# Four graph layers on one core: layer 1's steps moved by nearly half a period in the written order, the setup split into thirteen placed steps, new orders at both ends

## The chip, the core and the metric

The kernel runs on one core of a Trainium2 chip. The core has a matrix engine (TensorE, PE in the profile; its weight loads are listed as PEld), a vector engine (VectorE, DVE), a scalar engine with function tables (ScalarE, ACT), a general engine (GpSimd, POOL) and SyncE (SP), which here only issues DMA transfers. [...] The metric is the time of one execution on the device in microseconds, as the median of several runs.

## The reference

There are 64 graphs of 256 nodes with 256 features, `x` (64, 256, 256), and an adjacency matrix `adj` of 0 and 1. Four layers follow each other; after each, the sum of input and output is normalized (`_layernorm(x + layer(x))`). Cut to what matters:

```
# layer 0: attention with 4 heads, mask by adj, output projection, layer norm
q, k, v = x @ Wq.T + bq, x @ Wk.T + bk, x @ Wv.T + bv
attn = softmax(where(adj == 0, NEG, q k^T / 8));  out = norm((attn v) @ Wo.T + bo) * gamma + beta
# layer 1: 8 heads whose queries, keys and values are all norm(x), then a two-layer MLP
n = norm(x) * gamma1 + beta1;  x = x + softmax(mask(n n^T / sqrt(32))) n
x = x + gelu((norm(x) * gamma2 + beta2) @ W1 + b1) @ W2 + b2        # W1 is 256 x 1024
# layer 2: Wh = h @ W; scores leaky_relu(s1_i + s2_j), masked softmax, times Wh
# layer 3: scores leaky_relu((h * a0) h^T) where adj == 1, masked softmax, times h
```

## The kernel before

The 64 graphs are worked in 32 groups of two (`G = 2`). The work of a group is written as eleven Python generators, the threads, each of which issues a few instructions and then yields:

- `a` (`thread_a`, L686): loads adjacency and features; ACT makes a bf16 copy `adjb` and a check (`adjb`, `adj`), SP transposes it with four DMA transposes (`adjT`), DVE makes `mask` and the transposed `xT`; then layer 0's projections on PE (`WqT`, `WkT`, `WvT`), the scores (`ps<-qT,kT`, in two row tiles of 64), the exps on ACT (`e<-ps`), the masking on DVE, the products (`pm<-e,v`, in four column tiles of 32) and the row sums (`pm<-ea,ones`), whose reciprocal `zs` DVE takes.
- `u0`, `u1` (L798, one per graph): `zs` goes by DMA to memory (`lines`) and comes back spread over the partitions (`rr`); DVE scales `oT`, PE applies `WoT`, then two normalizations give `z`, layer 1's input, and `xb`.
- `z0`, `z1` (L850): `z` transposed, by a way through memory (`rows`, `blk`, then a DVE transposition into `t`), or on PE where `DIRECT` (L44) names it for a group.
- `b` (L857): layer 1's attention. Its scores are `ps<-t`, in four row tiles of 32; its exps are masked in quarters with a sum; its products are `pm<-e,z`, in four column tiles.
- `w0`, `w1` (L923): normalization, residual and transposition (`yT`).
- `c` (L964): W1 (`pm<-t,L_gnn_W`) and GELU on ACT (`hT<-pm`), in four pairs.
- `o0`, `o1` (L1009): W2 (`pm<-L_gnn_W,hT`), then layers 2 and 3 (`wx`, `ex`, `v,q`, then `pm<-t`, `q`, `xn,q`) and the output.

Which thread goes on next is written by hand. `PLACES` (L46) gives every step a place in periods; group g's copy of it is shifted by g, and all are sorted into one order (L1178). A period is 163 steps. The first 520 steps are replaced by the text `FIRST`, the last 444 by `LAST`: letter and digit are thread and group (counted from eight before the end in `LAST`). The class `InOrder` (L464) ties each instruction to the one recorded before it on its engine, so the written order is the order on every engine; all these instructions carry the line of that helper, L473. ACT's function tables follow from this order too: exp and GELU are in different sets, and the program holds an `ACT_TABLE_LOAD` wherever one follows the other.

Tiles come from pools that reuse a fixed number of buffers (`BUFS`, L45), each waiting for the last reader of what it held. In PSUM there are two score tiles `ps` and four tiles `pm` for everything else.

Constants: six loads stand on ACT's queue at the start. The other seventeen are collected in `later` (L532) and issued on SP by `prepare` (L1090), which runs beside the threads, one step after each of the seven turns in `PREPARE`: two steps with loads; `bop` = Wo applied to the value bias, plus `bo` (needs `WoT`, `bv`, `bo`); the loads of W1 and W2 with the sums for layer 2's vector (`wa`, `wx`); `b2m`; bounds for a check; and last the W1 step, in which PE multiplies W1 with `beta2` (16 products of one column, `pm<-beta,L_gnn_W`) and DVE scales W1 with `gamma2`. Small constants share the buffer of `hT` until group 0's GELU takes it.

Of the kernel before, what the change touches and what calls it, by code (L numbers as in the profile page):

```python
# [8 lines left out]
F32 = mybir.dt.float32  # L9
# [4 lines left out]
ALU = mybir.AluOpType  # L14
AX = mybir.AxisListType

P = 128
N = 256
D = 256
NC = D // P  # L20
# [4 lines left out]
W = D + 4  # L25
DFF = 1024
NF = DFF // P
EPS = 1e-5
SLOPE = 0.2
# [14 lines left out]
DIRECT = {0: ('x', 'z'), 31: ('yT', 'n2', 'n3')}  # L44
BUFS = {'t': 6, 'q': 3, 'k': 2, 'v': 5, 'y': 4, 'z': 4, 'xb': 4, 'both': 2, 'xn': 6, 'mask': 3, 'e': 6, 'x0': 2, 'turned': 1, 'blk': 3, 'oT': 2, 'zs': 2, 'rr': 2, 'xT': 1, 'qT': 1, 'kT': 1}  # L45
PLACES = {  # L46
    "a": (0.00000, 0.26380, 0.44172, 0.77301, 0.77914, 0.78528, 0.80982, 0.85890, 0.87730, 0.95092, 0.96932,
        0.99386, 1.04295, 1.07362, 1.08589, 1.11043, 1.12883, 1.13497, 1.17178, 1.18405, 1.19018, 1.21472,
        1.25767, 1.27607, 1.28221, 1.29448, 1.31902,),
    "u0": (1.33742, 1.34356, 1.34969, 1.40491, 1.41104, 1.49080, 1.54601, 1.56442, 1.60736, 1.68098,),  # L50
    "u1": (1.36810, 1.41718, 1.51534, 1.55215, 1.57055, 1.60123, 1.63190, 1.65031, 1.67485, 1.79141,),
    "z0": (1.61350, 1.66258, 1.69325, 1.72393,),
    "z1": (1.75460, 1.80368, 1.82209, 1.85276,),
    "b": (1.74847, 1.76074, 1.76687, 1.81595, 1.84049, 1.84663, 1.89571, 1.90184, 1.90797, 1.91411, 1.92024,
        1.92638, 1.93865, 1.95705, 1.96319, 1.98773,),
    "w0": (1.93251, 1.94478, 2.01841, 2.02454, 2.06135, 2.14110, 2.22086, 2.30675,),
    "w1": (2.01227, 2.03068, 2.03681, 2.09203, 2.14724, 2.20245, 2.23313, 2.31288,),
    "c": (2.32515, 2.38037, 2.48466, 2.50920, 2.53374, 2.57669, 2.58896, 2.61963,),
    "o0": (2.63804, 2.65644, 2.69939, 2.73620, 2.82822, 2.86503, 2.88957, 3.04908, 3.19632, 3.20859, 3.30061,
        3.33129, 3.37423, 3.38650, 3.39264, 3.42331, 3.43558, 3.46626, 3.47853, 3.52147, 3.58282, 3.62577,  # L60
        3.64417, 3.66871, 3.71779, 3.98159, 4.05521, 4.07975, 4.09816, 4.10429, 4.11656, 4.12270, 4.25153,
        4.59509,),
    "o1": (2.79755, 2.83436, 2.87117, 2.88344, 2.97546, 3.00614, 3.06749, 3.23926, 3.26994, 3.28834, 3.35583,
        3.36196, 3.42945, 3.44785, 3.45399, 3.46012, 3.47239, 3.49693, 3.50307, 3.55828, 3.68712, 3.70552,
        3.71166, 3.73006, 3.74233, 4.15337, 4.15951, 4.16564, 4.17791, 4.22699, 4.24540, 4.52761, 4.53988,
        5.39877,),
}
PREPARE = (8, 14, 26, 50, 70, 85, 100)
FIRST = (
    "a0a0a0a0a0a0a1a1a1a0a0a0a0a0a0a0a0a1a1a0a0a2a0a0a0a0a0a0a0a0a1a0a0a0U0U0U0a1a1U0a1u0u0a2U0U0u0u0U0U0U0Z0Z0u0"  # L70
    "u0u0u0a2Z0Z0U0b0b0b0b0u0z0b0a2z0z0b0z0b0b0b0b0b0b0W0W0a1b0b0b0a1b0a1W0W0W0W0w0u0w0w0w0W0a1a1a1a1a1a1a1a1a1a1"
    "W0a1w0a1a1a1w0w0w0c0a1c0U1U1c0c0U1U1u1U1U1u1u1c0a2a2c0c0c0u1O0O0U1U1U1Z1a2u1Z1u1U1u1u1O0u1o0O0Z1z1z1Z1b1b1b1"
    "O0z1o0o0o0u1z1b1b1b1a2a2b1b1b1b1b1b1O0O0W1W1b1o0a2b1b1a3a3a2a2b1o0O0a2w1W1W1W1o0o0w1w1w1a2a2a3a2a2a2a2a2W1W1"
    "a2a2w1w1w1O0O0a2a2a2W1o0a4o0U2U2w1a2a2u2u2o0o0c1c1O0O0o0o0o0o0o0c1u2c1o0o0o0U2O0O0O0O0U2c1O0O0O0U2U2c1U2U2O0"
    "O0c1c1u2U2Z2O1o0o0o0O1Z2u2u2O0O0o0a3o1U2O0u2u2o0Z2Z2u2O0O1O1z2a3a3b2b2b2o1o1o1a4z2z2b2b2b2z2a3a3a3b2b2b2b2b2"
    "b2b2b2a4a4O0O0W2O1O1W2O1a3a3b2b2o1o0o0a3a3o1W2W2w2W2W2u2w2w2O1w2O0O0a3a3a3a3o1a3W2W2O0O0w2w2w2a3a3a3a3O1o0o0"
    "o1o0o0O1a3a3a3U3U3o1o1a3w2O1a3c2O1U3o1c2o1O1O1O0O0U3U3U3u3u3u3o0o0o1o1o1o1c2c2O1U3U3c2c2O1O1u3U3Z3o1c2u3u3O1"
    "u3u3c2O1O2O2Z3o1u3Z3Z3O1O1u3b3o1o1O1O2O2z3o1O1O1o2O1O0b3b3b3o1o1z3b3O2z3O2O2o1o1b3o2o2a4z3b3a4b3a4O2b3b3b3b3"
    "b3o2a4a4O1O1b3O1O1a4a4W3b3a4U3W3W3W3o2b3w3o2o2O1a4a4a4a4w3w3a5W3O1w3")
LAST = (  # L80
    "a7w5a6o4o3o3O4O3a6a6a6W5W5o4a6o4o4U6U6w5a6u6u6c5c5o4O4U6o4o4o4O4o2o4o4U6U6U6o4o3c5c5c5O4o3O3c5a7o4o4U6U6U6Z6"
    "u6O4O4O4O4O4u6u6u6o4o4c5u6Z6u6c5O5Z6U6Z6b6O4O4o4O4u6z6z6O5b6b6b6u6O5O5O4z6b6o5b6O5O4O4O4o5a7o4o4a7a7z6b6o5o5"
    "b6a7b6b6b6b6W6W6b6a7a7b6a7a7W6W6O5O5b6b6o4o4o5o5o5a7w6w6w6O5a7a7a7a7O4w6a7a7O4O4O4W6W6a7a7a7w6w6o4O5o4o5O4O5"
    "a7a7O4a7a7W6o5o4o4W6w6w6o5o4a7U7o5U7a7U7o5u7u7c6c6U7O5o4o5O4O4U7O5c6u7c6U7o5o5U7U7U7Z7o5u7u7o3O5u7o5o5Z7O5O5"
    "O5u7u7Z7c6o5c6U7c6O5c6u7z7o5o5O6O6O6O5O6z7z7Z7b7b7o6b7b7u7o5O6O5O5O5b7b7O6O5o6o6o6z7b7O6b7b7O4b7b7W7b7O6W7o6"
    "o6o6b7b7o5o5O5O5O5b7b7w7O6W7O6o6w7o5o6o5o5o5w7W7o6O5W7o5o5w7O5w7o4O5o5W7W7O5O5O5O5w7w7O6w7W7c7c7O6O6o6O6O6o6"
    "c7c7o5O6O6c7O5O5o6o6o6o5o6c7c7c7o6o6O7O6O7O7O6O6o7o6O6O6O6O6O7O7o6o6o7o6O6o7O7O7o6o6O6O6o7o7O6O6O7O7o7O6o6O7"
    "O7O6o7o7O6o7o5o7o7O7o7O7O7O6O6O7O7O7o7o7o6o7o7o7o6o6o6o6o6O7o6O7O7O7o7o7O7o7o7o7O7O7O7o7o7o7O7O7O7o6O7O7o7o7"
    "O7o7O7O7o7o7o7o7O7o7o6o7")
LETTERS = dict(a="a", U="u0", u="u1", Z="z0", z="z1", b="b", W="w0", w="w1", c="c", O="o0", o="o1")  # L90
# [358 lines left out]
def usual_input(ctx: ExitStack, tc: tile.TileContext, a: dict, out: bass.AP, flag: bass.AP):  # L449
# [84 lines left out]
    def load(queue, to, of):  # L534
        if queue:
            queue.dma_start(to, of)
        else:
            later.append((to, of))

    def load_rows(name, cols, queue=None):  # L540

        src = a[name]
        t = const.tile([P, src.shape[0] // P, cols], F32, name=name)
        load(queue, t, src.rearrange("(c p) f -> p c f", p=P))
        return t
# [22 lines left out]
    beta0 = load_all(a["L0_gnn_beta"], "beta0", queue=ACT)  # L568
    woT = load_rows("L0_gnn_WoT", D)
    bv = load_column(a["L0_gnn_bv"], D, "bv")  # L570
    bo = load_all(a["L0_gnn_bo"], "bo", 0)

# [4 lines left out]
    gamma0 = load_all(a["L0_gnn_gamma"], "gamma0")  # L577
    beta1r = load_all(a["L1_gnn_beta1"], "beta1r")
    gamma1r = load_all(a["L1_gnn_gamma1"], "gamma1r", 256)
    b2 = load_all(a["L1_gnn_b2"], "b2", 512)  # L580
    gamma1 = load_column(a["L1_gnn_gamma1"], D, "gamma1")
    beta1 = load_column(a["L1_gnn_beta1"], D, "beta1")
    gamma2 = load_column(a["L1_gnn_gamma2"], D, "gamma2")
    beta2 = load_column(a["L1_gnn_beta2"], D, "beta2")
    b1 = load_column(a["L1_gnn_b1"], DFF, "b1")
    a0 = load_column(a["L3_gnn_a0"], D, "a0")
    w1 = load_rows("L1_gnn_W1", DFF)
    w2 = load_rows("L1_gnn_W2", D)
# [500 lines left out]

    def prepare():  # L1090

        for to, of in later[:3]:
            SP.dma_start(to, of)
        yield
        for to, of in later[3:-2]:
            SP.dma_start(to, of)
        yield
# [8 lines left out]
        for to, of in later[-2:]:  # L1106
            SP.dma_start(to, of)
        wa = setup[:, 1280:2304].rearrange("p (s c d) -> p s c d", s=2, c=NC)
        for s in range(2):
            DVE.tensor_tensor(wa[:, s], wx[:, :, 0:D], a12[:, s:s + 1, :].to_broadcast([P, NC, D]), ALU.mult)  # L1110
        DVE.tensor_reduce(wa1, wa, AX.X, ALU.add)
        for k, (s, share) in enumerate(((0, SLOPE - 1.0), (1, SLOPE), (1, 1.0))):
            DVE.tensor_scalar(wx[:, :, D + k:D + k + 1], wa1[:, s, :].unsqueeze(2), share, None, ALU.mult)

        yield
# [15 lines left out]

        yield
# [23 lines left out]
        yield  # L1156

        pm = new(ps_m, [P, NF], F32, "pm", 4)
        for f in range(NF):
            for c in range(NC):  # L1160
                matmul(pm[:, f:f + 1], w1[:, c, f * P:(f + 1) * P], beta2[:, c:c + 1], start=c == 0, stop=c == NC - 1)
        DVE.tensor_tensor(b1, b1, pm, ALU.add)
        for c in range(NC):
            DVE.tensor_scalar(w1[:, c, :], w1[:, c, :], gamma2[:, c:c + 1], None, ALU.mult)
# [7 lines left out]

    def written(text, since):
        return [(since + int(text[k + 1]), LETTERS[text[k]]) for k in range(0, len(text), 2)]

    preparing = prepare()
    groups = [threads_of(g) for g in range(B // G)]
    plan = [(g, n) for _, g, n in sorted((g + t, g, n) for g in range(B // G) for n, ts in PLACES.items() for t in ts)]  # L1178
    head, tail = written(FIRST, 0), written(LAST, B // G - 8)
    for turn, (g, name) in enumerate(head + plan[len(head):len(plan) - len(tail)] + tail):  # L1180
        next(groups[g][name], END)
        if turn in PREPARE:
            next(preparing, END)
    assert next(preparing, END) == END
# [54 lines left out]
```

## Time and profile before

| | before |
|---|---|
| median of three runs | 2473.54 us (2472.14 to 2473.80) |
| the profiled execution | 2474.4 us, span from first to last instruction 2472.5 us |
| PE busy | 2414.1 us (98%), 15888 instructions |
| DVE busy | 2119.0 us (86%) |
| ACT busy | 1510.2 us (61%), among it 65 table loads of 1283 ns |
| POOL busy | 747.2 us (30%) |
| DMA | 229.78 MB, mean 93 GB/s |

How to read it. The page divides the span into 40 slices of 61.8 us and gives each engine's busy share in tenths; PEclk is the share of its full clock that TensorE was granted. Every fp32 matmul of the program appears as two passes, so 16 products are `x32`. A matmul's shape is given as rows * columns of the array and as the size of what streams through: `128*128 128x256` fills the array, `32*128` is one of four row tiles, `128*32` one of four column tiles. Matmul lengths overlap, so durations on PE are best taken from start to start. In a list of waits the columns are who waited, for whom, microseconds in total, times, and the longest. A PE wait is listed only from 0.15 us on.

### The profile page before, as it was taken

Reading aid. Unit: us, or ns where it says so; the run is one execution under the profiler, and the core shown is the slowest. Engines: PE = TensorE matmul, PEld = TensorE weight load, DVE = VectorE, ACT = ScalarE, POOL = GpSimd, SP = SyncE. Lnnn points to the kernel's source line nnn. Section 1 sums busy time; section 2 is a strip of 40 time slices with the busy share of each in tenths; the row PEclk is TensorE's granted clock in tenths of the full one; section 3 lists DMA queues with packets and bytes.
Section 4 is the critical chain, followed back from the end, with each engine's and each line's share of the span. In section 5 each row is a group of like instructions: output and inputs, shape, how many; then the busy total and the mean of one; then the engine's idle time right before and its main releaser. Section 6 shows DMA issues by size and latency. Waiting matters only on the chain.

```text
span 2472.5 us, 48109 instructions
## 1 busy us (share of the span) xinstructions
PE 2414.1 (98%) x15888; PEld 1811.9 (73%) x15888; DVE 2119.0 (86%) x6238; ACT 1510.2 (61%) x2635; POOL 747.2 (30%) x1804
## 2 busy tenths in 40 slices
PE   5899999999999999999999999999999999999997
PEld 3577777777777777787777777777777777777776
DVE  4788888988888988889988889988888988889884
ACT  3456566666666666666666666665666666666654
POOL 0222233323233233233232333232333232333232
PEclk9899999999999999999999999999999999999999
DMA  6235253444443444443444444444444444434321
GB/s 143 46 82 108 61 112 88 92 98 101 96 103 86 92 97 101 101 103 86 91 96 102 103 96 91 89 99 103 103 87 96 92 99 101 106 85 92 81 65 44
DMA packets 903791, 229.78 MB, mean 93 GB/s; under 512 B 707313, under 2 KB 903153, under 8 KB 903537
## 3 DMA queue, kind: packets, MB, share of 16 engines
q1 hardware_dynamic: 902032, 225.73, 41.8%
q8 instruction: 128, 2.10, 0.4%
q14 instruction: 127, 1.03, 0.1%
q10 hardware_dynamic: 1504, 0.92, 0.1%
HBM read 136.07 MB, written 82.05 MB: 88 GB/s over the span
## 4 chain that ended last, share of the span: by engine, by line
PE 72%; ACT 8%; DVE 6%; DMA 5%; SPq 4%; POOL 3%; issue 2%; ACTq 0%; DVEq 0%; POOLq 0%
PE pm L473 65%; PE ps L473 7%; SPq L473 4%; DMA blk<-rows 3%; ACT e L473 2%; ACT adj L473 1%; DVE y L473 1%; DVE e L473 1%; ACT adjb L473 1%; POOL rstd L473 1%; ACT xn L473 1%; DVE st L473 1%; ACT xb L473 1%; POOL nm L473 1%; ACT oT L473 1%
## 5 line engine op out<-in xcount | busy, mean ns | idle before, releaser
L473 POOL TENSOR_SCALAR ve<-mv 128x2 f32<-128x2 f32 x448 | 149.3, 333 | 1613.9 <-DVE mv L473 1104.9
L473 PE MATMUL pm<-L_gnn_W,hT 128*128 128x256 f32 x2048 | 468.0, 382 | 0.0
L473 PE MATMUL pm<-t,L_gnn_W 128*128 128x256 f32 x2048 | 458.2, 379 | 1.6 <-DVE t L473 1.6
L473 ACT ACTIVATE e<-ps 128x1024 f32<-128x1024 f32 x384 | 373.0, 1021 | 126.1 <-PE ps L473 125.4
L473 PEld LDWEIGHTS pm<-L_gnn_W,hT 128*128 128x128 f32 x2048 | 382.0, 190 | 67.0 <-issue 18.9
L473 PEld LDWEIGHTS pm<-t,L_gnn_W 128*128 128x128 f32 x2048 | 386.5, 190 | 53.9 <-DVE t L473 2.1
L473 DVE SCALAR_TENSOR_TENSOR e<-e,mask 128x256 f32<-128x256 f32 x1024 | 364.7, 420 | 12.7 <-ACT e L473 12.4
L473 POOL TENSOR_TENSOR rstd<-ve,mhalf 128x2 f32<-128x2 f32 (+1 forms) x384 | 344.9, 898 | 32.0
L473 ACT ACTIVATE xn<-y,nm,rstd 128x256 f32<-128x256 f32 x256 | 139.5, 593 | 278.0 <-POOL xn L473 223.0
L473 DVE BATCH_NORM_STATS2 st<-y 128x6 f32<-128x256 f32 x640 | 236.3, 411 | 4.7
L473 DVE STREAM_TRANSPOSE t<-blk 128x512 f32<-128x512 f32 x248 | 172.1, 703 | 75.1 <-DMA blk<-rows 74.9
L473 ACT ACTIVATE hT<-pm,b 128x512 f32<-128x512 f32 x256 | 163.9, 676 | 28.5 <-PE pm L473 25.1
L473 PE MATMUL ps<-t 32*128 32x256 f32 x2048 | 156.8, 406 | 5.2 <-ACT t L473 4.0
L473 DVE TENSOR_TENSOR e<-e,mask 128x1024 f32<-128x1024 f32 x128 | 149.7, 1213 | 0.5 <-ACT e L473 0.5
L473 PEld LDWEIGHTS ps<-t 32*128 32x128 f32 x2048 | 100.7, 187 | 61.1 <-ACT qT L473 18.9
L473 DVE SCALAR_TENSOR_TENSOR y<-pm,r,xn 128x256 f32<-128x256 f32 x256 | 123.8, 484 | 9.4
L473 PE MATMUL pm<-wx,t 128*128 128x259 f32 x512 | 127.7, 392 | 2.4
L473 PE MATMUL ps<-qT,kT 64*128 64x256 f32 x1024 | 129.4, 393 | 0.5 <-ACT e L473 0.5
L473 PE MATMUL pm<-e,v 128*32 128x256 f32 x2048 | 125.9, 386 | 2.2
L473 PE MATMUL pm<-e,z 128*32 128x256 f32 x2048 | 127.5, 385 | 0.1
L473 PE MATMUL pm<-xn,q 128*128 128x257 f32 x512 | 127.0, 380 | 0.0
L473 ACT COPY v<-pm 128x259 f32<-128x259 f32 (+1 forms) x192 | 81.3, 442 | 71.9 <-PE pm L473 71.9
(133 smaller groups left out, 4207.5 us busy)
## 6 DMA issues: line engine op xcount, KB each, us to landing
blk<-rows SPq DMA_DIRECT2D x992, 64.0 KB
rows<-xn SPq DMA_DIRECT2D x248, 128.0 KB
x<-in_x SPq DMA_DIRECT2D x32, 512.0 KB
adj<-in_adj SPq DMA_DIRECT2D x32, 512.0 KB
rr<-lines SPq DMA_DIRECT2D x128, 128.0 KB
out<-xn SPq DMA_DIRECT2D x64, 256.0 KB
turned<-in_x SPq DMA_DIRECT2D x248, 64.0 KB
rows<-xb SPq DMA_DIRECT2D x124, 128.0 KB
```

The costliest lines, as they stand in the source:

```text
L473: ins = call(*args, **kw)
```

## The change

- `PLACES` is new in all its lines. In the old one, threads `u`, `z` and `b` of a group run up to 1.99 periods after its start, in the new one up to 2.73; with them `w`, `c` and `o` begin later, and the last step is at 5.70 instead of 5.40. Within one period, layer 1's scores stood between W2 blocks and the projections of the group after; now the first of them stand next to layer 0's products.
- `FIRST` has 581 steps instead of 520, `LAST` 536 instead of 444.
- The setup has its own letters: `l` for eight steps of loads (`loading`, new) and `p` for five steps of arithmetic (`prepare`, without loads). They have places in `FIRST` like any other step. W1 and W2 are loaded in two halves each, ahead of the first `lines`; the loads of `wx`, `a`, `gamma1r` and `a0` come last. The W1 step moves from seventh to second place, `wa` after `b2m`, and the bounds to the end. In `FIRST`, group 1's adjacency conversion and transposes move from ahead of group 0's projections to after its products.
- `BUFS`: `t` 6 to 5, `v` 5 to 4, `both` 2 to 3, `mask` 3 to 4. `DIRECT` names `'o'` for groups 0 and 31; only `thread_w` asks for it, and there only if `FO` is true, which it is not.

In the diff below, the new texts are cut to their first lines.

```diff
-DIRECT = {0: ('x', 'z'), 31: ('yT', 'n2', 'n3')}
-BUFS = {'t': 6, 'q': 3, 'k': 2, 'v': 5, 'y': 4, 'z': 4, 'xb': 4, 'both': 2, 'xn': 6, 'mask': 3, ...
+DIRECT = {0: ('x', 'z', 'o'), 31: ('yT', 'n2', 'n3', 'o')}
+BUFS = {'t': 5, 'q': 3, 'k': 2, 'v': 4, 'y': 4, 'z': 4, 'xb': 4, 'both': 3, 'xn': 6, 'mask': 4, ...
 PLACES = {
-    "b": (1.74847, 1.76074, 1.76687, 1.81595, 1.84049, 1.84663, 1.89571, 1.90184, 1.90797, 1.91411, 1.92024,
-        1.92638, 1.93865, 1.95705, 1.96319, 1.98773,),
-    "c": (2.32515, 2.38037, 2.48466, 2.50920, 2.53374, 2.57669, 2.58896, 2.61963,),
+    "b": (2.12270, 2.15951, 2.22086, 2.22699, 2.35583, 2.36196, 2.43558, 2.46626, 2.47239, 2.47853, 2.48466,
+        2.49080, 2.51534, 2.58896, 2.65031, 2.73006,),
+    "c": (3.18405, 3.23313, 3.26380, 3.27607, 3.34969, 3.37423, 3.41104, 3.46012,),
...
-PREPARE = (8, 14, 26, 50, 70, 85, 100)
 FIRST = (
-    "a0a0a0a0a0a0a1a1a1a0a0a0a0a0a0a0a0a1a1a0a0a2a0a0a0a0a0a0a0a0a1a0a0a0U0U0U0a1a1U0a1u0u0a2U0U0u0u0U0U0U0Z0Z0u0"
+    "a0a0a0a1a0a0a0a0a0a0a0l0l0l0a0a0a0a0l0l0a0a0a0a0a0a0a0l0l0a0a0a0a0U0U0a1a0a0a2p0U0U0U0u0U0U0U0U0a1u0u0p0u0a1"
+    "a1a1u0u0l0a2a1Z0a1a1Z0a1Z0Z0u0u0u0U0a3p0p0a1a2a2a2u0a1a1a1a1a1a1a1a1a1a1a1z0z0z0b0b0z0a1a1a1a2U1U1b0a1a1u1b0"
...
-            later.append((to, of))
+            later[-1].append((to, of))
...
+    def loading():
+        for some in later:
+            for to, of in some:
+                SP.dma_start(to, of)
+            yield
+
     def prepare():
-        for to, of in later[:3]:
-            SP.dma_start(to, of)
-        yield
-        for to, of in later[3:-2]:
-            SP.dma_start(to, of)
-        yield
...
+        pm = new(ps_m, [P, NF], F32, "pm", 4)
+        for f in range(NF):
+            for c in range(NC):
+                matmul(pm[:, f:f + 1], w1[:, c, f * P:(f + 1) * P], beta2[:, c:c + 1], start=c == 0, stop=c == NC - 1)
+        DVE.tensor_tensor(b1, b1, pm, ALU.add)
+        for c in range(NC):
+            DVE.tensor_scalar(w1[:, c, :], w1[:, c, :], gamma2[:, c:c + 1], None, ALU.mult)
         yield
...
-    for turn, (g, name) in enumerate(head + plan[len(head):len(plan) - len(tail)] + tail):
+    groups[0].update(l=loading(), p=prepare())
+    since = sum(n not in "lp" for _, n in head)
+    for g, name in head + plan[since:len(plan) - len(tail)] + tail:
         next(groups[g][name], END)
-        if turn in PREPARE:
-            next(preparing, END)
```

## The prediction, made before the changed kernel ran

> **What bounds the kernel now.** I read the page first, then the busy time by stretches, then who TensorE waited for, then TensorE's instructions in order of time.
>
> ```profile
> span 2472.5 us, 48109 instructions
> ...
> PE   5899999999999999999999999999999999999997
> ...
> PEclk9899999999999999999999999999999999999999
> ```
>
> TensorE (PE) is full in 37 of 40 slices and below full at both ends only; its granted clock too is below full only at the start. The stretches put numbers on that (columns: window, its length, busy time of PE, PEld, DVE, ACT, POOL with counts, clock, DMA share, GB/s):
>
> ```profile
> 0.00:60.00 60.00, 36.81 (x180) 20.08 (x180) 23.04 (x35) 20.10 (x33) 2.58 (x13) 0.91 0.58 141
> 60.00:126.00 66.00, 54.00 (x384) 37.34 (x385) 49.84 (x153) 31.33 (x48) 14.70 (x24) 0.84 0.26 49
> 126.00:2300.00 2174.00, 2167.63 (x14385) 1634.58 (x14384) 1919.58 (x5648) 1365.79 (x2380) 683.50 (x1624) 1.00 0.44 96
> 2300.00:2461.00 161.00, 154.77 (x941) 119.43 (x939) 123.40 (x390) 90.82 (x171) 43.30 (x132) 1.00 0.26 59
> ```
>
> Three regimes. Up to 126 us PE is idle 23.2 + 12.0 = 35.2 us and runs at a reduced clock. From 126 to 2300 it is busy 2167.6 of 2174 us; the waits reported there add up to 1.4 us. From 2300 to 2461, before the final checks, 6.2 us are lost. Head waits by releaser:
>
> ```profile
> PE pm L473 <- DVE ea L473: 6.5, 3, 4.5
> PE pm L473 <- DMA x<-in_x: 6.0, 1, 6.0
> PE pm L473 <- ACT z L473: 4.8, 1, 4.8
> PE pm L473 <- ACT xT L473: 3.6, 1, 3.6
> ```
>
> A busy PE may still be slow. One steady period lasts 74.50 us (the WqT block starts at 1038.77, the next at 1113.27). Its order of time (start, length, engine, what, count):
>
> ```profile
> 1028.01 1.47 PE L473 MATMUL pm<-t 128*128 128x256 f32 x8
> 1029.41 1.15 PE L473 MATMUL ps<-t 32*128 32x256 f32 x16
> 1030.49 3.72 PE L473 MATMUL pm<-L_gnn_W,hT 128*128 128x256 f32 x16
> 1034.14 1.15 PE L473 MATMUL ps<-t 32*128 32x256 f32 x16
> 1035.22 3.72 PE L473 MATMUL pm<-L_gnn_W,hT 128*128 128x256 f32 x16
> 1038.77 3.60 PE L473 MATMUL pm<-xT,L_gnn_WqT 128*128 128x512 f32 x8
> 1042.30 1.15 PE L473 MATMUL ps<-t 32*128 32x256 f32 x16
> 1043.38 1.93 PE L473 MATMUL pm<-e,z 128*32 128x256 f32 x32
> 1045.24 1.37 PE L473 MATMUL ps<-t 32*128 32x256 f32 x16
> 1046.54 0.66 PE L473 MATMUL pm<-ident,oT 128*128 128x128 f32 x4
> ```
>
> Take starts, not lengths. Sixteen W2 passes (pm<-L_gnn_W,hT) between full-array neighbours take 3.45 us (1019.80 to 1023.25), 0.216 each; between two ps<-t blocks 3.65 (1030.49 to 1034.14). A ps<-t block, four concurrent sets, should take 4 x 0.216 = 0.86 and takes 1.08. So **a change between the full array and a tiled form costs time that counts as busy**.
>
> **What the Trainium skill says.** "TensorEngine Tiling (Array Packing)", Key Properties: a change of tiling mode, unlike a change of tile, drains TensorE. The trace agrees, and prices it: one visit full-rows-full costs about 0.2 in the neighbours and 0.2 in the block. "ScalarE: Activation LUTs", What ACT_TABLE_LOAD costs: 1283 ns and a drain of 1380, 2.66 us for every switch of set. The trace has the 1283 and not the drain:
>
> ```profile
> 1075.28 0.19 ACT L473 ACTIVATION_READ_ACCUMULATOR pm<-zs 128x1 f32 x1
> 1075.49 1.28 ACT L473 ACT_TABLE_LOAD   x1
> 1076.78 1.26 ACT L473 ACTIVATE hT<-pm,b 128x512 f32<-128x512 f32 x2
> ```
>
> so I take 1.28. "TensorE: Matmul & The Clock Gate", Part 1: after an idle window of about 3.4 us the clock is halved. The head agrees (clock 0.91 and 0.84, waits up to 6.0 us).
>
> **The change, part by part.** No matmul, vector or scalar arithmetic is added or removed; order and buffers change.
>
> *Places.* I laid one period's PE steps of both place lists in order and marked each as full (F), row-tiled (R: q-k scores, layer 1 scores) or column-tiled (C: e,v and e,z). Before: eight visits from F, two direct R-C changes. After, layer 1's scores lie beside layer 0's products (R-C, then C-R) and its own chain R-C-R stays: six visits, four direct changes. Prices from start-to-start times in the steady part: last F pass before a tiled block +0.09; first set of a block +0.10 (R) or +0.02 (C); last set +0.10 to 0.11; first F pass after +0.05 to 0.10. Hence about 0.38 a visit and 0.20 a direct change; per period 3.16 before and 2.81 after, **0.35 less**. Over both whole orders, the written ends included: 250 visits and 64 direct changes before, 188 and 128 after; -62 x 0.38 + 64 x 0.20 = **-10.5 us**. All of it lies on the path, since PE waits for nothing there.
>
> *Waits too short for the reports.* The period holds stalls: the score block at 1045.24 takes 1.30 instead of 1.08 (it waits for score tiles that the exps hold), and three steps around wx and ea 0.1 to 0.16 too much: 0.63 us a period, 28 periods, 17 us. In the new order the score block meets exps that follow at once, but GELU comes just ahead of them. I take -3; bounds -16 (all vanish) and +8 (half as much again).
>
> *ACT table loads.* The layer 1 exps now interleave with the four GELU pairs: four loads a period instead of two; 68 more in the instruction order, 68 x 1.28 = 87 us, ACT from 61 to 65%. I cost them at nothing: following ACT's queue by hand with these durations, the second tile of layer 1's first scores is free 1.3 us before PE needs it, the later tiles 0.5 us or more. If that cover goes, each us late is paid in every period.
>
> *Buffers.* t 6 to 5, v 5 to 4; both and mask one more. By the steps, each t and v is read last at least 17 steps of 163 before its reuse: nothing, either way. The 'o' in DIRECT is read only where FO is true; it is false: nothing.
>
> *Head.* Before, group 1's adjacency conversion stands on ACT ahead of group 0's qT, its four transposes on SP (5.0 us) ahead of the constants, and the bop matmuls ahead of the first products. After, group 0 goes first. From durations before: v matmuls 1.8 us earlier (22.2 to 20.4); products at 28.5 instead of 35.0, as bop's operands are not awaited; zs at 34.3 and 37.8 instead of 41.1 and 49.0. Fifteen constant loads stand ahead of lines on SP with w1 and w2, 2.7 MB from 15.5 us; at the 353 GB/s of 55 to 60 us, or half, gone by 23 to 31. lines and rr then take 2.0 + 0.7 + 2.9 us (the unburdened second pair), so oT at 40, z at 51.4, and group 1's projections start at 54.4, 10.4 us of full-array work that covers z's way. Waits up to there: 6.0 + 3.6 as before, then 0.3 + 1.2 + 0.6 + 2.1 + 1.8 + 3.0 + 0.8 + 1.9 = 21 us; after it DVE, near full, costs 4 to 8. So 27 idle against 35.2: -8. The clock cost 5.4 x 0.6 + 10.6 x 0.8 = 12 us before; dense work from 54 on saves perhaps 4. **Head -12**, bounds -3 (DVE holds PE later instead) and -22. The moved steps: the wa, bounds and b2m sums (DVE 5.8 us; POOL a memset and a power) and the w1 step (32 small passes, 3.6 us of PE, into an idle stretch; DVE 1.5) go past group 1's statistics on DVE and POOL; unloaded by then, nothing, or 2 us if late. The last load step's four DMAs follow group 1's turned x.
>
> *Tail.* The same last blocks in nearly the same order; the final values, normalization and output stay. 0, bounds -4 and +4.
>
> Sum: 2474.4 (the profiled execution: span 2472.5 and 1.9 around it) - 10.5 - 3 - 12 = 2448.9; the median of the runs is 0.9 lower, so **2448**.
>
> **Rivals.** (1) The switches do save, but new short waits eat it: the head alone, 2473.5 - 12 = 2461. For: DVE is busy 88% in the middle, and walking its queue leaves ea only 0.5 us ahead of its matmuls. (2) All short waits vanish and the head gives 20: 2473.5 - 10.5 - 16 - 20 = 2427. For: the paired order separates the two demands on score tiles. (3) Slower: ACT, in strict order, reaches layer 1's exps late, as they stand behind a copy that waits for DVE's reciprocal and between two table loads. It decides when the lateness exceeds the 1.3 us of cover by 22.5 / 28 = 0.8 us; with both extra loads uncovered, (2.56 - 1.3) x 28 = 35 us, 2451 + 35 = 2486. Against it: ACT has a third of the period free. (4) The new order moves waits without shortening anything: 2472.
>
> **How the numbers follow.** Main case 0.58 (own range 2440 to 2456), (1) 0.17 (2457 to 2467), (2) 0.14 (2422 to 2439), (3) 0.08 (above 2479), (4) 0.03. The range 2431 to 2466 leaves out (3), (4) and the lower part of (2), 0.18. A measurement of this kernel can tell about 0.2% from no change, 5 us: faster 0.89, same 0.04, slower 0.07.
>
> **What would show it.** Right: a period near 74.1; six visits in it; no listed PE wait between 130 and 2300 above 2 us in sum; about 133 table loads; PE idle below 30 us up to 126; group 1's WqT at about 54. Wrong: a period at or above 74.5, PE waiting for ACT e in each period, or constants that delay lines. 1 us a period in listed waits would overturn the sign.

## The result, and the profile after

| | before | after |
|---|---|---|
| median of four runs | 2473.47 us (2472.14 to 2473.80) | 2437.62 us (2437.33 to 2439.34) |
| the profiled execution | 2474.4 us, span 2472.5 us | 2437.9 us, span 2436.0 us |
| TensorE busy | 2414.1 us | 2393.9 us |
| one steady period | 74.50 us | 73.83 us |
| TensorE idle, whole span / up to 126 us | 58.4 / 35.2 us | 42.1 / 24.9 us |

The ratio is 0.9858, 95% interval 0.984 to 0.9875. The forecast of 2448.0 us was 10.4 us too high, within its range of 2431 to 2466, but below the main case's own range (2440 to 2456). The page of the changed kernel has the same shape; only its first slices are fuller:

```profile
span 2436.0 us, 47812 instructions
...
PE   7899999999999999999999999999999999999997
...
PEclk8999999999999999999999999999999999999999
```

The busy time by stretches (window, its length, busy time of PE, PEld, DVE, ACT, POOL, clock, DMA share, GB/s):

```profile
0.00:60.00 60.00, 44.18 (x217) 29.06 (x218) 26.57 (x45) 20.86 (x34) 7.60 (x19) 0.86 0.53 148
60.00:126.00 66.00, 56.88 (x471) 35.63 (x469) 60.10 (x172) 39.16 (x63) 12.40 (x24) 0.97 0.32 71
126.00:2300.00 2174.00, 2172.50 (x14528) 1650.03 (x14520) 1935.01 (x5738) 1449.62 (x2461) 633.53 (x1640) 1.00 0.45 96
```

In the first 60 us PE works 7.4 us more than before (44.18 against 36.81), in the next 66 us 2.9 more. In the middle it has only 1.5 us free instead of 6.4, although the listed waits there hardly changed (1.3 us against 1.4): the rest were gaps below the 0.15 us from which a wait is listed. In the head, these waits lead now:

```profile
PE pm L474 <- DMA x<-in_x: 6.2, 1, 6.2
PE pm L474 <- DVE oT L474: 5.0, 2, 3.3
PE ps L474 <- ACT e L474: 4.2, 5, 2.0
```

The 6.5 us for DVE ea and the 4.8 us for ACT z are gone or halved (ea 3.3). Now PE in order of time in one steady period, around layer 0's products:

```profile
1067.75 2.02 PE L474 MATMUL pm<-wx,t 128*128 128x259 f32 x8
1069.70 1.15 PE L474 MATMUL ps<-t 32*128 32x256 f32 x16
1070.77 1.93 PE L474 MATMUL pm<-e,v 128*32 128x256 f32 x32
1072.52 0.61 PE L474 MATMUL pm<-ea,ones 128*32 128x256 f32 x8
1073.07 3.72 PE L474 MATMUL pm<-t,L_gnn_W 128*128 128x256 f32 x16
```

Layer 1's scores (ps<-t) stand directly ahead of e,v: a row-tiled block beside a column-tiled one, as the place lists had it. Behind the products of the first graph now follows a W1 block of 3.65 us. Before, it was a wx block:

```profile
1067.86 0.72 PE L473 MATMUL pm<-ea,ones 128*32 128x256 f32 x8
1068.67 1.99 PE L473 MATMUL pm<-wx,t 128*128 128x259 f32 x8
...
1070.73 1.93 PE L473 MATMUL pm<-e,v 128*32 128x256 f32 x32
```

From start to start, ea,ones took 0.81 us before and takes 0.55 now (1072.52 to 1073.07), and wx into a tiled block 2.06 against 1.95 (1067.75 to 1069.70). These are the short stalls that no list shows. What ended them in the kernel before stands in the queues of the other two engines: wx (1068.67) started behind DVE's reciprocal r, which ended at 1068.57, and the second e,v (1070.73) behind ACT's copy of oT, which ended at 1070.68.

```profile
1068.44 0.13 DVE L473 RECIPROCAL r<-pm 128x1 f32<-128x1 f32 x1
1070.12 0.56 ACT L473 COPY oT<-pm 128x512 f32<-128x512 f32 x1
```

In the changed kernel that copy comes while the W1 block runs, a microsecond before the second e,v:

```profile
1075.10 0.56 ACT L474 COPY oT<-pm 128x512 f32<-128x512 f32 x1
```

### The profile page after: what moved, and what is told of

It reads as the page before. It is cut to its first block, busy times and chain, and to the rows that moved or that the text cites. A ratio compares the mean times of both kernels' runs of the same rounds, so it can differ in the third digit from the quotient of the medians.

```text
span 2436.0 us, 47812 instructions
## 1 busy us (share of the span) xinstructions
PE 2393.9 (98%) x15888; PEld 1813.0 (74%) x15888; DVE 2108.3 (87%) x6238; ACT 1588.5 (65%) x2703; POOL 689.8 (28%) x1804
## 4 chain that ended last, share of the span: by engine, by line
PE 91%; DVE 4%; ACT 2%; DMA 1%; POOL 1%; issue 1%; SPq 0%; DVEq 0%; POOLq 0%; ACTq 0%
PE pm L474 81%; PE ps L474 10%; DVE e L474 1%; DVE y L474 1%; DVE zs L474 0%; DVE st L474 0%; POOL rstd L474 0%; SPq L474 0%; ACT L474 0%; DMA blk<-rows 0%; DMA adj<-in_adj 0%; ACT e L474 0%; POOL nm L474 0%; DMA rows<-xn 0%; ACT xn L474 0%
## 5 line engine op out<-in xcount | busy, mean ns | idle before, releaser
L474 POOL TENSOR_SCALAR ve<-mv 128x2 f32<-128x2 f32 x448 | 155.5, 347 | 1652.5 <-DVE mv L474 1455.5
L474 PE MATMUL pm<-L_gnn_W,hT 128*128 128x256 f32 x2048 | 453.5, 379 | 0.5 <-ACT hT L474 0.5
L474 PEld LDWEIGHTS pm<-t,L_gnn_W 128*128 128x128 f32 x2048 | 383.6, 190 | 63.4 <-ACT xn L474 10.3
L474 POOL TENSOR_TENSOR rstd<-ve,mhalf 128x2 f32<-128x2 f32 (+1 forms) x384 | 317.0, 826 | 32.1 <-POOL ve L474 0.2
L474 ACT ACTIVATE hT<-pm,b 128x512 f32<-128x512 f32 x256 | 169.6, 682 | 67.2 <-PE pm L474 66.5
L474 ACT ACTIVATE xb<-y,nm,rstd 128x256 f32<-128x256 f32 x128 | 69.5, 591 | 148.1 <-DVE both L474 136.7
L474 ACT ACTIVATE xn<-y,nm,rstd 128x256 f32<-128x256 f32 x256 | 138.4, 591 | 20.3 <-POOL xn L474 12.6
L474 PE MATMUL pm<-L_gnn_WoT,oT 128*128 128x256 f32 x512 | 126.4, 392 | 5.1 <-DVE oT L474 5.0
L474 PE MATMUL pm<-v,q 128*128 128x260 f32 x512 | 130.6, 389 | 0.5 <-DVE r L474 0.5
```

The lines of the kernel that those rows point to most:

```text
L474: ins = call(*args, **kw)
```

## Where the 36.5 us came from

I split the difference of the two spans by the trace: head and tail by PE's idle time and by the half-clock stretches of the clock records (half of the busy time in them is lost; the first 15 us, ahead of the first record, are counted as half clock, since WqT takes 5.63 us there and 3.60 later); the steady part by comparing the period block by block.

| term | forecast | measured |
|---|---|---|
| mode switches, steady periods | most of -10.5 | 24 x 0.30 = -7.2 |
| short stalls, steady periods | -3 | 24 x 0.37 = -8.9 |
| head, up to 126 us | -12 | idle -10.3, clock -3.0: -13.3 |
| tail | 0 | idle -0.9, clock +1.6: +0.7 |
| the same switches and stalls outside the steady periods | the rest of -10.5 | -7.8 (by difference) |
| sum of the span | -25.5 | -36.5 |

The forecast counted 28 periods; between the WqT blocks of groups 6 and 30, both traces have 24 that are steady. The stalls' 0.37 a period is ea,ones 0.80 to 0.55 and wx 2.07 to 1.95, medians over 17 periods; the switches' 0.30 is what remains of 74.50 - 73.83 = 0.67. Of the last row, 2.2 us are periods of up to 75.1 us that the kernel before has among its 24. Another 2.1 us is an estimate from the forecast's counts and prices: 14 of the 62 visits and 16 of the 64 direct changes lie outside the steady periods. The rest is not taken apart.

## The experiments

**Head and places, each alone.** Two hybrids, the other half of the written order taken from the kernel before:

```diff
-PLACES = { ... }, LAST = ( ... )        # of the changed kernel
+PLACES = { ... }, LAST = ( ... )        # of the kernel before; FIRST and setup stay
+    rest = list(plan)                   # the middle is the plan without what head and tail hold
```

> The changed kernel's head (its FIRST, its setup steps, its buffers) with the places and the LAST of the kernel before. Theory (head and period are separate gains, head about 12 us by idle time and clock): idle of TensorE up to 126 us near 25 us, a steady period of 74.50 us as before, time 2473.5 - 12 = 2461 us (2458 to 2466, as the seam between head and places may cost some us). Rival (the head's gain is given back later, all of the gain is in the period): 2473 us.

Measured 2472.61 us (2470.85 to 2474.09; ratio 0.9992, 0.9984 to 1.0). Neither number of the theory: by the total alone, the rival. The stretches say otherwise. Idle time up to 126 us is 22.6 us, the period 74.50; but from 250 to 400 us, where the new head meets the old places, PE loses 9.7 us (before: 0.35), 8.4 of them in one wait for DVE r:

```profile
250.00:400.00 150.00, 140.28 (x948) 106.82 (x945) 118.71 (x363) 90.98 (x158) 42.16 (x105) 0.97 0.35 77
```

The clock's loss is 18.6 us instead of 15.5. So the head's 12.6 us of idle time are there, and the seam takes them back: by the step counts the new head ends with groups 4 and 5 further on, and groups 1 to 3 less far, than the old places expect.

> The head and setup of the kernel before with the places, the LAST and the buffers of the changed kernel. Theory: a steady period of 73.83 us, idle up to 126 us near 35 us, time 2473.5 - 24 = 2449.5 us (2446 to 2455, seam included). Rival (head decides what follows): near 2438 or near 2473 us.

Measured 2476.00 us (2473.13 to 2479.51; ratio 1.0008, 0.9999 to 1.0016). Again the seam: 16.4 us of idle time from 250 to 400 us, and a clock loss of 21.8 us. The period is 73.82 us, idle up to 126 us 36.9. My allowance of a few us for a seam was wrong in both runs, so their totals decide nothing; the periods and the head's idle time agree with the theory. What these two runs do show is that the gain needs head and places of one kind.

**A visit more.** In the changed kernel, one step moved:

```diff
-    "o0": (... 4.13497, 4.24540, 4.25153, ...   # the two transposes of ex
+    "o0": (... 4.13497, 4.22393, 4.25153, ...
```

> The changed kernel with one step, the two transposes of ex (0.25 us, full array), placed between layer 0's second products and layer 1's second scores: in each period one direct change between tiled forms becomes a visit of its own, nothing else. Theory (a visit 0.38 us, a direct change 0.20): period 73.83 + 0.18 = 74.01 us, time 2437.6 + 28 x 0.18 = 2442.7 us. Rival (neighbourhood saves nothing, the gain of the period was all stalls): 2437.6 us.

Measured 2444.23 us (2443.02 to 2446.11), period 74.04 us. Block by block, the two transposes take 0.36 between tiled blocks against 0.27, and the W1 block behind the scores 3.56 against 3.46: 0.19 a period from the blocks that changed, as priced. The total is 6.6 us longer, of which 24 x 0.21 = 5.0 by the periods' lengths; one more stretch of half clock, at 117 us, adds 1.9. The switch prices hold for this one exchange of a direct change for a visit.

**The stalls taken away in the kernel before.**

```diff
-    "a": (0.00000, 0.26380, ...            # adjacency conversion on ACT
+    "a": (0.00000, 0.27914, ...            # second run: 0.29141
-    "o0": (... 4.12270, 4.25153, ...       # statistics (DVE), normalization (ACT)
+    "o0": (... 4.24847, 4.37117, ...
```

> The kernel before with three steps placed later: the adjacency conversion on ACT behind the copy of oT of the first graph, and one step of statistics and its normalization in layer 2 behind the sums ea. No mode switch is added or removed. Theory (stalls under 0.15 us each, which no list of waits shows, are worth 0.42 us a period: ea,ones 0.11, the first wx after it 0.16, the e,v after that 0.15): period 74.08 us, time 2473.5 - 28 x 0.42 = 2462 us. Rival (these steps are slow for another reason, and only the switches count): period 74.50, time 2473.5 us.

Measured 2521.39 us (2521.09 to 2524.38; ratio 1.0195, 1.0181 to 1.0209), period 76.3 us: slower. The three stalls did go, ea,ones 0.80 to 0.54 and wx 2.07 to 1.95, but the transposes of ex now waited 1.35 us for ACT v, which stood behind the moved conversion, and the products after them 0.61 us longer for DVE q.

> As the run with three steps placed later, but the adjacency conversion on ACT stands behind the copies of layer 2's values and their exp as well, so that nothing which TensorE needs soon is queued behind it. Theory (the three short stalls are gone as in that run, and what it paid, 1.35 us of TensorE waiting for ACT v and 0.37 for DVE q in each period, goes too): period 74.08 us, time 2473.5 - 28 x 0.42 = 2462 us. Rival 1 (whatever ACT does with 2.3 us of conversion at this point, some later work waits for it): period above 74.5. Rival 2 (the short stalls are worth nothing): 2473.5 us.

Measured 2497.06 us (2495.05 to 2498.76; ratio 1.0092, 1.0075 to 1.0109), period 75.36: rival 1. One period of this run:

```profile
1076.02 0.61 PE L473 MATMUL pm<-ea,ones 128*32 128x256 f32 x8
1076.57 2.02 PE L473 MATMUL pm<-wx,t 128*128 128x259 f32 x8
...
1083.33 1.99 PE L473 MATMUL pm<-t,L_gnn_W 128*128 128x256 f32 x8 [0.32 <-ACT oT L473]
...
1086.80 1.12 PE L473 MATMUL pm<-v,q 128*128 128x260 f32 x4 [0.38 <-DVE q L473]
```

Against the kernel before: -0.26 at ea,ones, -0.12 at wx, then +0.58 at W1, whose second tile waits for the copy of oT behind the conversion, and +0.61 at v,q. So the stalls are real and of the size read, 0.38 us a period, but with these moves the engines that cause them pass them on to the next block. I found no order of the kernel before that removes them unpaid.

**The cover in the changed kernel.** There, by the trace, the wx block that waited for r no longer stands behind the first products, and the W1 block in its place covers the way to the second ones.

```diff
-    "c": (3.18405, 3.23313, ...            # first W1 block
+    "c": (3.22945, 3.23313, ...
```

> The changed kernel with one step moved: the first W1 block of layer 1 (3.65 us of TensorE), which stands between layer 0's products of the first and the second graph, goes behind the second's. Theory (this block is what covers DVE's and ACT's way to the second products: oT is copied by 1075.7, the sums ea are there at 1077.3, and without the block TensorE would ask for them at 1073.1 and 1074.8): one visit to a tiled form less, -0.38, and a wait for DVE ea of about 2.4 us in each period; period 75.8 us, time 2437.6 + 28 x 2.0 = 2494 us (2480 to 2500). Rival (neighbourhood of tiled blocks is what gains, cover matters little): period 73.45, time 2427 us.

Measured 2553.56 us (2550.63 to 2554.80; ratio 1.0312, 1.0298 to 1.0326), median period 78.6. The direction and the wait are the theory's, the size is not:

```profile
1195.86 1.91 PE L474 MATMUL pm<-e,v 128*32 128x256 f32 x32
1199.71 1.14 PE L474 MATMUL pm<-ea,ones 128*32 128x256 f32 x8 [1.94 <-DVE ea L474]
1200.78 2.09 PE L474 MATMUL ps<-t 32*128 32x256 f32 x16
```

The wait for DVE ea is 1.94 us (24 such waits from 400 to 2250 us, 46.7 us in sum), and the moved W1 block and the step behind it add 0.39 and 0.67, the latter a listed wait of 0.56 for ACT hT. The rest is the clock: behind the wait, the same score block takes 2.02 us instead of 1.08, start to start. The clock records have 19 such stretches of 3.41 us at half clock between 340 and 2222 us, where the changed kernel has none; they cost 32 us. So this block is what covers DVE and ACT, and without it the kernel is 116 us slower, twice the 56 expected.

**Table loads.**

```diff
-                ACT.activation(hT[:, f, :], pms[f % 2], AF.Gelu, bias=b1[:, f:f + 1])
+                ACT.activation(hT[:, f, :], pms[f % 2], AF.Identity, bias=b1[:, f:f + 1])
```

> The changed kernel with Identity in place of GELU (this leaves GELU out of the computation), so that ACT keeps one table and nearly all of the 133 table loads disappear, 68 of which the change added. Theory (loads lie in idle time of ACT): period 73.83 us within 0.05, time 2437.6 us within 2. Rival (part of the loads delays scores or products, and the change would have gained more without them): several us less, 2.56 us a period at most.

Measured 2439.02 us (2436.82 to 2439.61), period 73.83, one table load instead of 133. Hidden, as costed. In the changed kernel ACT waits for the scores with the load already done:

```profile
1021.28 1.28 ACT L474 ACT_TABLE_LOAD   x1
1023.37 1.94 ACT L474 ACTIVATE e<-ps 128x1024 f32<-128x1024 f32 x2 [0.81 <-PE ps L474]
```

Without the load, the same exps wait 2.11 us for the same scores.

**The head undone, step by step.** In the changed `FIRST`, group 1's steps put back:

```diff
-    "a0a0a0a1a0a0a0a0a0a0...U0U0a1a0a0a2p0...
+    "a0a0a0a1a0a0a0a1a1a0a0a0...U0U0a0a0a2p0...     # second run: p0 ahead of the first products too
```

> The changed kernel with group 1's adjacency conversion (ACT) and transposes (SP) put back ahead of group 0's projections, as in the kernel before; all else as changed. Theory: group 0's v products wait 1.8 us for ACT, the constants leave SP 10 us later and lines by some 2 us, later work is a little earlier; TensorE's idle time up to 126 us 2 to 4 us above the 24.9, the period unchanged at 73.83, time 2440.5 us (2438 to 2443). Rival (this move was no part of the head's gain): 2437.6 us or less.

Measured 2444.93 us (2443.44 to 2446.27): +7.3, more than the 3 expected. Idle up to 126 us is 30.1 us (+5.2), the clock's loss 1.7 us more. The SP queue of the changed kernel, then of this one:

```profile
34.75 0.65 SPq L474 DMA_DIRECT2D lines<-zs  x1
36.47 1.30 SPq L474 DMA_DIRECT2D rr<-lines  x2
```

```profile
20.49 5.04 SPq L474 DMA_TRANSPOSE adjT<-adjb  x4
...
38.33 0.65 SPq L474 DMA_DIRECT2D lines<-zs  x1
42.27 1.30 SPq L474 DMA_DIRECT2D rr<-lines  x2
```

lines goes 3.6 us later: 1.8 by ACT, since zs ends at 36.6 instead of 34.7, and 1.8 because the constants occupy SP up to 38.2. Then rr follows after 3.9 us instead of 1.7, as lines lands behind the weights that are still moving (some 250 GB/s from 38 to 42 us; under 10 around 35 us in the changed kernel). DVE multiplies oT by rr at 46.16 instead of 40.59. I had counted the queue and not the slower landing.

> As the run before it, and the products that make bop put ahead of group 0's first attention products, as in the kernel before. Theory: their operands, issued from 25.4 us, land near 33 us, so that the attention products start near 35 us instead of 28.4; idle up to 126 us near 33, period 73.83, time 2437.6 + 8 = 2445.5 us (2442 to 2449). Rival (a head delay is made good by later work, TensorE then waits less for the same chain): 2440 us or less.

Measured 2444.30 us (2443.29 to 2444.76): the rival. The attention products do start at 34.09 instead of 30.25 us, but lines leaves at 38.34 as in the run before: there the constants held SP up to 38.2, here zs is ready at 38.3. Behind the constants, the place of bop costs nothing; with the constants out of the way it was not tried alone.

**The W1 step.**

```diff
-    ...u1.2, p.1 (W1 step), u1.3 (Wo), ..., k products, ..., p.2
+    ...u1.2, u1.3 (Wo), ..., k products, ..., p.1 (W1 step), p.2
```

> The changed kernel with the W1 step (32 products of one column on TensorE, three operations on DVE) moved from the gap behind group 0's first Wo product to behind group 1's k products. Theory (where the change put it, TensorE waited anyway, so it cost nothing; behind full-array work it stands on the path): 3.5 us of TensorE more, less what DVE's 1.5 us give back earlier; idle up to 126 us a little above 24.9, time 2437.6 + 3.5 = 2441 us (2439 to 2445). Rival (TensorE waits for DVE's chain later in the head anyway, and the step is hidden in either place): 2437.6 us within 1.5.

Measured 2444.39 us (2443.65 to 2444.84): +6.8. First the changed kernel, then this one:

```profile
44.98 6.83 PE L474 MATMUL pm<-beta,L_gnn_W 128*128 128x1 f32 x32
```

```profile
51.60 3.78 PE L474 MATMUL pm<-L_gnn_WoT,oT 128*128 128x256 f32 x8 [6.02 <-DVE oT L474]
```

In the gap the step took 6.83 us at half clock and nobody waited for it: group 1's q products start at 56.2 us, and at 56.1 in this run. Moved, it costs 3.5 us between k and v, and idle up to 126 us is 28.5 us. The clock adds to it. Both kernels have 17.1 us of half clock from 40 us on, whether the gap is filled or empty. But this run then has 3.4 us more at 68, straight behind the moved step, where TensorE had not paused; the v products take 5.3 us there instead of 3.55:

```profile
63.82 3.63 PE L474 MATMUL pm<-beta,L_gnn_W 128*128 128x1 f32 x32
67.31 5.39 PE L474 MATMUL pm<-L_gnn_WvT,xT 128*128 128x256 f32 x16
```

It also has 6.8 us at 88 and 6.8 at 119, against 3.4 at 84; both begin in or just behind waits that the changed kernel has too (3.3 us for DVE oT, 1.7 to 2.0 for ACT e), and why they are longer stays open. The clock's loss is 4.4 us larger in all, 1.0 of it in the first 17 us, where both kernels still do the same. The theory's 3.5 held for the work and missed the clock.

**Group 1's projections into the gap.** The head above suggested filling it:

```diff
-  P1, a2.0, p.0, u0.2, u0.3 (Wo), ..., p.1 (W1 step), ..., a1.3 (x), a1.4, a1.5, ..., z, q, k, ...
+  a1.1, v0, ..., a1.2, a1.3 (x), P0, P1, lines, rr, ..., a1.4, u0.2, u0.3 (Wo), a1.5, p.0, q, k, Wo, v, z, ...; p.1 later
```

> The changed kernel with another order of its first 102 written steps: group 1's adjacency conversion stands on ACT between group 0's kT and v copies, its transposes and its x ahead of group 0's lines on SP (W2's loads move behind rr), and its q, k and v products on TensorE between group 0's two Wo products and z, in place of the W1 step, which moves behind group 1's first attention products. Theory (the head waits for the chain zs, lines, rr, oT, z, and what it lacks is other work in that gap): about 8.7 us of projections fill it, idle up to 126 us falls from 24.9 to near 18, the clock's loss from 14 to near 9, period 73.83; time 2437.6 - 10 = 2427.6 us (2422 to 2433). Rival (the statistics on DVE are next in line and hold group 1's products later by as much): 2437.6 us within 2.

Measured 2448.26 us (2443.71 to 2449.90; ratio 0.9901, 0.9885 to 0.9916): 10.6 us slower than the changed kernel, worse than the rival. q and k do fill 47.0 to 53.9 us, but oT waits 6.1 us ahead of them (rr is issued 3.3 us after lines, which lands behind x), the second scores of group 1 wait 3.9 us for ACT e, and the W1 step, now at 77.4 us, takes 6.99 us on the path. Idle up to 126 us is 30.8, the clock's loss 18.8. No version here beats the changed kernel.

**Buffers.** In the kernel before:

```diff
-BUFS = {'t': 6, ... 'v': 5, ...
+BUFS = {'t': 5, ... 'v': 4, ...
```

> The kernel before with t on five buffers instead of six and v on four instead of five, as the change has them. Theory (each is read last at least 17 of 163 steps before its buffer is taken again): period 74.50, time 2473.5 us within 2. Rival (a wait for the last reader appears on ACT or DVE): period above 74.5, time above 2478 us.

Measured 2472.79 us (2471.26 to 2474.54; ratio 1.0, 0.9992 to 1.0008). Nothing, as costed.

## Why the prediction was nearly right

- **Mode switches, -10.5.** Right in the period. The prices held in the split run (0.19 against 0.18 a period), the period has six visits, and 0.30 of the period's 0.67 us is left for them against the 0.35 forecast. The sum itself, -62 x 0.38 + 64 x 0.20, comes to -10.8.
- **Waits too short for the reports, -3.** This is the term that was mis-sized. Its stalls were read rightly in sum (0.37 us a period where 0.42 was read), but in two places instead of three (ea,ones 0.80 against 0.55, wx 2.07 against 1.95), and I took them as mostly replaced by new ones. In the new period only the score block (1.30 instead of 1.08) is left, and -8.9 us came from the steady periods alone. The step that failed was to look for what the new order adds at the score tiles, and not for what follows each stalled block. Behind the first products stood wx, 1.95 us of work that itself started late; now W1 stands there, 3.65 us, longer than the lateness of DVE and ACT. The run without this cover shows that it counts, and the two runs on the old order show that moving the late work instead doesn't help. That wx is no longer late, the larger part with 0.25 us, is read from the traces and from these two runs, in which that stall went; no run puts wx back.
- **Table loads, 0.** Right, and shown by taking them away.
- **Buffers, 0.** Right, for t and v.
- **Head, -12.** The sum was nearly right (-13.3), the reasons in part. The products at 28.41 and zs at 34.7 and 38.4 came as worked out; oT at 40.6 too. But z came at 54.6 instead of 51.4, in large part since the Wo block ahead of it ran at half clock (3.75 us instead of 1.89), and group 1's q products at 56.2 instead of 54.4. What carries the gain is group 1's adjacency work out of the way (7.3 us) and the W1 step in the gap (6.8 us when moved out of it); bop's place did not count behind the constants. These undone pieces do not add up to the head's gain, as each was taken alone. Idle time fell by 10.3 instead of 8, the clock's loss by 3.0 instead of 4.
- **Tail, 0.** Nearly right, +0.7: 0.9 us less idle time, and 1.6 more lost by the clock, with a stretch of half clock at 2412 us that the kernel before does not have. Its switches and stalls are in the row by difference.
- **Rivals.** The time falls into the range given to (2), 2422 to 2439, at its upper end. But (2) let all short waits vanish (-16, against -8.9 in the steady periods) and gave the head 20 (against 13.3), and the score block's wait is still there; the terms are the main case's, with the stalls larger. (1) and (4) are too high; against (3) stands the run without GELU, too.

## What to carry to other kernels

When a bound engine shows steps that are a tenth of a microsecond too long, list them by start-to-start times and ask of each which block the new order puts behind it: a longer neighbour hides the lateness in every period, while moving the late instruction handed it to the next block in both runs here. Price a change at the head by the chain and by the queue of transfers ahead of it, then add the clock, which here fell behind long waits and behind a block of one-column products alike. Two written orders that fit their own pipelines cannot be halved and recombined cheaply.

## What the runs showed of the hardware

- A wait of TensorE of 1.94 us was followed by 3.41 us at half clock in 19 of the periods of the run without the cover, and not in every one. The Trainium skill ("TensorE: Matmul & The Clock Gate", Part 1) names at least one idle window of about 3.4 us as the condition; here a gap of little more than half of it was enough. Periods with such a stretch took 78.6 us, the others 77.0.
- TensorE need not pause for the clock to fall. The stretches of the clock records are multiples of 3.41 us. In six traces, the kernel before among them, the 3.41 us ahead of a half-clock stretch held no pause and 2.3 us or more of the W1 step's one-column products; where they held at most 2.2 us of them, again without a pause, full clock went on.
- A product of one column is not cheap: the 32 passes of the W1 step took 3.5 us between full-array blocks, 0.11 each, half of the 0.216 of a pass with 256 columns.
- lines and rr, 4 KB and 128 KB, take 1.7 us from one issue to the next when the queues are quiet (under 10 GB/s) and 3.9 us behind the loads of the weights (some 250 GB/s).
